# Two bites of TensorE in the short steps of the late attention, and scatters three in two steps

## The chip, the cores and the metric

The kernel runs on one core of a Trainium2 chip. The metric is the device time of one execution in microseconds, as the median of several runs. A core has five engines with queues of their own: TensorE (matmuls), VectorE, ScalarE, GpSimd (POOL) and SyncE (SP, which here only issues DMAs). They meet through semaphores alone.

## The reference

Four batches of 1024 tokens with 256 features go through four blocks in a row, each with a layer norm in front and added to its input: attention, a mixture of experts, a short convolution over the batch axis, and the mixture of experts again.

```python
x = x + attn(layernorm(x))     # 16 heads of 16; scores ** 4, causal, divided by their sum
x = x + ffn(layernorm(x))      # top 6 of 16 experts (176 wide), and a shared expert (352 wide)
x = x + conv(layernorm(x))     # taps from delta, alpha, beta, gamma; silu
x = x + ffn(layernorm(x))

# attn, for each head
a = tril(einsum('bhnd,bhmd->bhnm', q, k) ** 4)      # q, k: rotary, then a layer norm over the head
out = einsum('bhnm,bhmd->bhnd', a / a.sum(-1), v)
```

All is float32.

## The kernel before

**Tiling.** Tokens stand in tiles of 128 (`X`: 8 tiles by 4 batches). The experts' tokens form two groups: the first four tiles of every batch are group 0, the last four group 1. For each group a plan picks the experts (`plan`, line 324); a scatter (`scatter`, line 420) writes each token's normed row six times into a queue in DRAM (`xq`), sorted by expert, one indirect DMA of POOL (line 445) for 128 rows; then 111 tiles of that queue run through the experts (`stream`, line 1047), and the results are gathered back (line 1217). Group 0's queue is filled for the first time while the attention still runs.

**The attention.** It runs in 16 passes: first the queries 0 to 511 (`hf` 0) of eight pairs (four batches by two groups of eight heads), then the queries 512 to 1023 (`hf` 1) of the same eight. A pass has two halves `a` of four heads, and each half runs over the blocks of 128 keys, in the order of `turns` (line 856): 0, 3, 1, 2 for the first queries, and 0, 7, 1, 6, 2, 5, 3, 4 for the second. So there are 8 x 8 + 8 x 16 = 192 steps. A step has one block of keys `j` against at most 512 queries; behind the diagonal there are fewer, in the second half 384, 256 and 128 for `j` 5, 6 and 7.

In each step the loop (line 888) first issues the scores of the step two ahead (`scores`, line 719: four matmuls at line 727, two squarings on ScalarE at line 738, masks and the second power of one part on VectorE, lines 745 and 758); then the second power of the other part on ScalarE (line 896); then this step's weighing of the values (`weigh`, line 765: four matmuls at line 773, into one accumulator). A matmul of float32 shows as two in the profile, so a step has eight of line 727 and eight of line 773.

**Bites.** All other work of the attention is cut into generators, which stand in five lanes (`Bites`, line 45): two for the projection, rotation and norm of queries, keys and values of a pass to come, one for the layer norm and transposes of its input, one for the outputs (`gather_bites`, `project_bites`), and one, ROUTE, for the zero fill of the queues and then for the routing of group 0: logits, plan and scatters. A generator yields "pe" ahead of a piece that uses TensorE, "el" ahead of one that doesn't, and "gap" where it is to wait for the next step. `step(pe, counts)` goes through the lanes in order, runs up to `counts` pieces of each, and at most `pe` with TensorE in all. It is called twice in a step of the loop: with one "pe" and one piece a lane ahead of the weighing, and behind it with the arguments that the change touches. `ran` counts the "pe" pieces, and is taken before the first call. A scatter is an "el" of its own, so a step issues at most as many scatters as the two calls let ROUTE have pieces. ROUTE's routing is added (line 918) once the first queries' outputs are through.

In the second half the second call had one "pe" only if the first had found none (line 907):

```python
                    pe = 1 if hf == 0 or bites.ran == ran else 0
                    bites.step(pe, (2, 2, 1, 2, 1))
```

**Order.** TensorE, VectorE, ScalarE and SP run their instructions in the order in which the program issues them (`manual_schedule`). POOL is not among these engines; it has the scatters, and in the second half the copies of the values into `vB` (line 611), two a pass. The rows to scatter are normed into `sxn` for two tokens' tiles (12 scatters) at a time (line 429, by way of line 207); the next 12's rows are made six scatters ahead, in one of two buffers.

**What follows.** At the end of the loop the last outputs are drained, then what is left of ROUTE. Then the memory of the attention is given to the experts' weights and buffers: the first rows of the shared expert (`hxn`, line 973), its transposes (`hpt`, line 985), the loads of the weights (lines 940 to 956) and of the queue (`xg`, line 1062).

Of the kernel before, what the change touches and what calls it, by code (L numbers as in the profile page):

```python
# [99 lines left out]
def chain(*parts):  # L100
    for part in parts:
        yield from part
# [3 lines left out]
def block_kernel(  # L106
# [154 lines left out]
    plans = {}  # L261
# [46 lines left out]
    def prepare_all(g, pool, ps):  # L308

        for i in range(TG):  # L310
            yield "el"
            ln_stats(X[:, g * TG + i, :, :], mvs[g][:, 4 * i : 4 * i + 4, :], "r")
        yield "gap"
        yield "el"
        ln_root(mvs[g], rstds[g])
        yield "gap"
        yield "el"
        nc.vector.reciprocal(rstds[g], rstds[g])
        for i in range(TG):
            if i:  # L320
                yield "el"
            yield from logits_of(g, i, pool, ps)
# [148 lines left out]
    with ExitStack() as actx:  # L471
# [65 lines left out]
        def zero_fill():  # L537
            for q in xq:
                rows = q.rearrange("(p r) e -> p r e", p=P)
                for c in range(0, NTILE, LB):  # L540
                    yield "el"
                    nc.sync.dma_start(
                        out=rows[:, c : c + LB, :],
                        in_=zero[:, None, :].to_broadcast([P, LB, E]),
                    )
# [7 lines left out]
        def norm_bites(l, hf):  # L553

            xs = X[:, 4 * hf : 4 * hf + 4, l, :]
            yield "el"
            mv = small.tile([P, 4, 2], FP, tag="a_mv", name="a_mv")
            rstd = small.tile([P, 4], FP, tag="a_rstd", name="a_rstd")
            ln_stats(xs, mv, "a")
            yield "gap"  # L560
            yield "el"
            ln_root(mv, rstd)
            yield "gap"
            yield "el"
            nc.vector.reciprocal(rstd, rstd)
            xn = ap1.tile([P, 4, E], FP, name="xn")
            ln_apply(xs, xn, mv, rstd)
            xnT = ap2.tile([P, 2, 512], FP, name="xnT")
            xnT_of[l, hf] = xnT
            yield "gap"  # L570
            yield "gap"
            for k in range(2):
                yield "pe"
                pt = ps_m().tile([P, 512], FP, tag="m", name="pt")
                transpose4(pt, xn, slice(k * P, (k + 1) * P))
                nc.scalar.copy(xnT[:, k, :], pt)
# [188 lines left out]
        def weigh(u, hf, a, j, last, s2s):  # L765
            n0 = max(0, (j - 4 * hf) * P)
            if j == 0:
                accs[0] = PS["a"].tile([P, 512], FP, tag="acc", name="acc")
            acc = accs[0]
            va = vs_of[u, j // 4]  # L770
            for r in (2, 0, 1, 3):
                h = 2 * r + a
                nc.tensor.matmul(  # L773
                    acc[32 * r : 32 * r + 32, n0:512],
                    lhsT=va[:, j % 4, h * VW : h * VW + 32],
                    rhs=s2s[r // 2][:, r % 2, 0 : 512 - n0],
                    start=(j == 0),
                    stop=(j == last),
                )
            if j == last:  # L780
                o_sb = ap2.tile([P, 4, P], FP, name="o_sb")
                nc.scalar.copy(o_sb.rearrange("p t n -> p (t n)"), acc)
                return o_sb

        def gather_bites(u, hf, a, o_sb):

            yield "gap"
            yield "pe"
            l, gp = pairs[u]
            if gp == 0 and a == 0:  # L790
                at_of[l, hf] = ap2.tile([P, 4, E], FP, name="at")
            at = at_of[l, hf]
            po = ps_m().tile([P, 4, G, 32], FP, tag="m", name="po")
            for i in range(4):
                nc.tensor.transpose(
                    po[:, i, :, :].rearrange("p r d -> p (r d)"), o_sb[:, i, :], ident
                )
            rd = small.tile([P, 4, G], FP, tag="rd", name="rd")
            nc.vector.reciprocal(rd, po[:, :, :, D])
            nc.vector.tensor_mul(  # L800
                at.rearrange("p t (g r a d) -> p t g r a d", g=2, r=G, a=2)[:, :, gp, :, a, :],
                po[:, :, :, 0:D],
                rd[:, :, :, None].to_broadcast([P, 4, G, D]),
            )
# [32 lines left out]
        bites = Bites(5)  # L837
# [3 lines left out]
        def begin_chain(n):  # L841

            hf, u = passes[n]
            l, gp = pairs[u]
            if gp == 0:
                bites.need(NORM, (l, hf))
            bites.add(gp, qkv_bites(u, hf), n)
            if gp == 1 and n + 1 < len(passes):
                hf, u = passes[n + 1]
                l = pairs[u][0]  # L850
                bites.add(NORM, norm_bites(l, hf), (l, hf))
# [12 lines left out]
        def forward(i):  # L864

            n, a, j, last = steps[i]
            hf, u = passes[n]
            if a == 0 and j == 0:
                bites.need(pairs[u][1], n)
            if hf == 0 and a == 1 and j == 0:  # L870
                begin_chain(n + 2)
            if hf == 1 and u > 0 and a == 0 and j == 0 and n + 1 < len(passes):
                begin_chain(n + 1)
            return scores(u, hf, a, j, last)

        with tc.manual_schedule(engines=ORDERED):
            with tc.tile_pool(name="ps_s", bufs=2, space=PSUM) as s, tc.tile_pool(
                name="ps_a", bufs=1, space=PSUM
            ) as a, tc.tile_pool(name="ps_m", bufs=3, space=PSUM) as m:
                PS.update(s=s, a=a, m=m)  # L880
                bites.add(NORM, norm_bites(0, 0), (0, 0))
                begin_chain(0)
                bites.need(QKV0, 0)
                begin_chain(1)
                bites.add(ROUTE, taps(ap1, ps_m))
                bites.add(ROUTE, zero_fill())
                routed = False
                for s in range(-LOOK, len(steps)):
                    bites.begin()
                    new = []  # L890
                    ran = bites.ran
                    if s + LOOK < len(steps):
                        powers[s + LOOK], new = forward(s + LOOK)
                    bites.step(1, (1, 1, 1, 1, 1))
                    for part in later:
                        nc.scalar.activation(part, part, AF.Square)  # L896
                    later[:] = new
                    if s < 0:
                        bites.step(1, (2, 2, 1, 2, 1))
                        continue  # L900
                    n, a, j, last = steps[s]
                    hf, u = passes[n]
                    o_sb = weigh(u, hf, a, j, last, powers.pop(s))
                    if a == 1 and j == last:
                        weighed[0] = n

                    pe = 1 if hf == 0 or bites.ran == ran else 0
                    bites.step(pe, (2, 2, 1, 2, 1))
                    if o_sb is not None:
                        l, gp = pairs[u]  # L910
                        done = gather_bites(u, hf, a, o_sb)
                        if gp == 1 and a == 1:
                            done = chain(done, project_bites(l, hf))
                        bites.add(OUT, done)
                    if hf == 1 and not routed and not bites.lanes[OUT]:

                        routed = True
                        bites.add(ROUTE, prepare_all(0, ap1, ps_m))
                        bites.add(ROUTE, chain(plan(0, ps_m), scatter(0, ap2, 1)))
                bites.drain(OUT)  # L920
                bites.drain(ROUTE)


    with ExitStack() as fctx:
# [120 lines left out]
        bites = Bites(3)  # L1045
# [344 lines left out]
```

## Time and profile before

| | us |
|---|---|
| median of 3 runs | 2450.68 (2448.94 to 2451.34) |
| profiled execution | 2440.91 |
| its span, first to last instruction | 2439.2 |
| TensorE busy in the span | 2133.4 (87%), 10512 matmuls |
| ScalarE busy | 1240.8 (51%) |
| VectorE busy | 1110.1 (46%) |
| POOL busy | 846.5 (35%) |
| line 445, 384 scatters | 384.1, 1.00 each |
| line 727, score matmuls, 1024 of the group with the first queries' keys | 167.8 |
| line 773, weighing, 1024 of the group with the first queries' values | 124.5 |
| first scatter of group 0, start | 554.4 |
| last scatter of group 0, start | 721.1 |
| last weighing, end | 711.6 |
| first experts' matmul (line 1091) | about 805 |

The page of a profile gives each engine's busy time in 40 slices, the chain of waits that ended last (followed back from the last instruction through what released each one), the groups of instructions by line, and the idle time before them with what ended it. "Another core or an unknown queue" stands where the release fits no instruction of the profile. The ends of matmuls are modelled, so a wait for TensorE beyond its last recorded end falls under that name. The attention ends at 711.6 us; the rest is the shared expert of group 0, four streams of 111 tiles, and the last combine.

### The profile page before, as it was taken

What the parts mean: (1) busy time and instruction counts of PE and PEld (TensorE: products, weight loads), DVE (VectorE), ACT (ScalarE), POOL (GpSimd) and SP (SyncE); (2) the same over time, 40 slices, a digit from 0 to 9 for tenths busy, and PEclk for the clock granted to TensorE, in tenths of its full rate; (3) what the DMA queues carried; (4) which work ended last, traced back from release to release, by engine and by line L of the source; (5) the groups of instructions that cost most, each with busy time, mean ns of one, the idle gap of its engine ahead of it and who ended that gap; (6) DMA issues with size and microseconds to landing.
All of it is one profiled execution on the core that took longest, in us unless ns stands there. A gap on an engine that the chain in (4) does not pass through costs nothing.

```text
span 2439.2 us, 32993 instructions
## 1 busy us (share of the span) xinstructions
PE 2133.4 (87%) x10512; PEld 1328.8 (54%) x10512; DVE 1110.1 (46%) x2599; ACT 1240.8 (51%) x2774; POOL 846.5 (35%) x903
## 2 busy tenths in 40 slices
PE   5899999997769988899899987988998799999755
PEld 2344433332225766677666655766665467777433
DVE  6888777884542341111465511146561113431244
ACT  4788888886651543345455423445552334555200
POOL 3222100006650026600554066155406625530365
PEclk8899999998889999999999998999999899999967
DMA  7900000002224134433444243344424336653233
GB/s 252 329 1 1 1 1 1 1 1 78 74 94 124 56 100 173 167 102 115 146 138 132 80 153 139 102 144 146 122 84 149 143 106 189 193 169 104 89 100 93
DMA packets 210214, 267.72 MB, mean 110 GB/s; under 512 B 23232, under 2 KB 185184, under 8 KB 210048
## 3 DMA queue, kind: packets, MB, share of 16 engines
q1 hardware_dynamic: 168544, 161.43, 20.5%
q0 software_dynamic: 37056, 100.91, 12.8%
q10 hardware_dynamic: 4448, 3.28, 0.5%
q8 instruction: 91, 1.49, 0.3%
q14 instruction: 75, 0.61, 0.1%
HBM read 123.72 MB, written 141.82 MB: 109 GB/s over the span
## 4 chain that ended last, share of the span: by engine, by line
PE 67%; DVE 15%; ACT 7%; another core or an unknown queue 6%; issue 4%; DMA 1%; POOL 0%; ACTq 0%; DVEq 0%; POOLq 0%
PE pgu L1091 19%; PE py L1114 15%; PE ps L727 5%; PE pht L1105 4%; PE pxt L1075 4%; PE pg L1010 3%; PE acc L773 3%; PE pu L1010 3%; PE pj L600 3%; PE po L1030 2%; DVE s L758 2%; ACT s L738 2%; DVE X L1201 1%; DVE s L745 1%
## 5 line engine op out<-in xcount | busy, mean ns | idle before, releaser
L1091 PE MATMUL pgu<-wgu,xgT 128*128 x1776 | 617.3, 471 | 4.5 <-DVE hbuf L1100 3.2
L1217 POOL DMA_INDIRECT yg<-yq,sloti x384 | 381.6, 994 | 589.4 <-DMA yq<-yo 325.5
L445 POOL DMA_INDIRECT xq<-sxn,sloti x384 | 384.1, 1000 | 517.1 <-ACT xgT L1077 362.9
L1100 DVE TENSOR_TENSOR hbuf<-hbuf,pgu 128x176 f32<-128x176 f32 x444 | 149.0, 336 | 746.4 <-ACT hbuf L1099 616.4
L1091 PEld LDWEIGHTS pgu<-wgu,xgT 128*128 128x128 f32 x1776 | 345.8, 196 | 140.8 <-issue 22.7
L1099 ACT ACTIVATE hbuf<-pgu 128x176 f32<-128x176 f32 x444 | 142.1, 320 | 393.3 <-PE pgu L1091 273.0
L738 ACT ACTIVATE s<-ps 128x1024 f32<-128x1024 f32 (+3 forms) x384 | 291.9, 816 | 83.4 <-PE ps L727 53.6
L1114 PE MATMUL py<-w2a,hT 128*128 x888 | 282.7, 401 | 35.3 <-issue 24.4
L1123 ACT COPY yo<-py 128x256 f32<-128x256 f32 x444 | 166.5, 375 | 250.9 <-PE py L1114 141.6
L1114 PE MATMUL py<-w2b,hT 128*128 x888 | 274.3, 392 | 0.0
L1105 PE MATMUL pht<-ident,hbuf 128*128 128x128 f32 x888 | 175.4, 280 | 64.6 <-ACT hT L1107 57.7
L1105 PEld LDWEIGHTS pht<-ident,hbuf 128*128 128x128 f32 x888 | 124.0, 144 | 195.8 <-ACT hT L1107 75.8
L758 DVE TENSOR_TENSOR s<-s 128x1024 f32<-128x1024 f32 (+3 forms) x176 | 177.8, 1010 | 74.0 <-ACT s L738 65.9
L1201 DVE SCALAR_TENSOR_TENSOR X<-yg,top,X 128x256 f32<-128x256 f32 x384 | 185.4, 483 | 42.5 <-DMA yg<-yq,sloti 33.4
L1077 ACT COPY xgT<-pxt 128x256 f32<-128x256 f32 x444 | 170.0, 383 | 41.0 <-remote 9.3
L1114 PEld LDWEIGHTS py<-w2b,hT 128*128 128x128 f32 x888 | 175.1, 197 | 25.5
L1107 ACT COPY hT<-pht 128x256 f32<-128x256 f32 x444 | 166.1, 374 | 35.6 <-PE py L1114 13.4
L727 PE MATMUL ps<-q,kA 32*128 32x512 f32 (+3 forms) x1024 | 167.8, 595 | 17.8 <-ACT s L738 7.6
L1075 PE MATMUL pxt<-ident,xg 128*128 128x128 f32 x888 | 174.5, 279 | 9.7 <-issue 5.3
L896 ACT ACTIVATE s<-s 128x1024 f32<-128x1024 f32 (+3 forms) x208 | 169.5, 824 | 15.1 <-DVE s L745 15.1
L1114 PEld LDWEIGHTS py<-w2a,hT 128*128 128x128 f32 x888 | 138.4, 196 | 48.1 <-issue 28.4
L773 PE MATMUL acc<-s,vA 128*32 128x512 f32 (+3 forms) x1024 | 124.5, 552 | 16.8 <-ACT s L896 14.5
(165 smaller groups left out, 2311.0 us busy)
## 6 DMA issues: line engine op xcount, KB each, us to landing
xg<-xq SPq DMA_DIRECT2D x148, 384.0 KB
yq<-yo SPq DMA_DIRECT2D x148, 384.0 KB
xq<-zero SPq DMA_DIRECT2D x74, 384.0 KB
xq<-sxn,sloti POOLq DMA_INDIRECT x384
yg<-yq,sloti POOLq DMA_INDIRECT x384
wgu<-in_w SPq DMA_DIRECT2D x4, 1408.0 KB
X<-in_x SPq DMA_DIRECT2D x8, 512.0 KB
out<-X SPq DMA_DIRECT2D x8, 512.0 KB
```

The costliest lines, as they stand in the source:

```text
L445: d = nc.gpsimd.indirect_dma_start(out=xq[g][:, :], out_offset=bass.IndirectOffsetOnAxis(ap=sloti[:, c + i, k : k + 1], axis=0), in_=xs[:, ...
L727: nc.tensor.matmul(tiles[h // 2][:, h % 2, 0:nq], lhsT=kt[32 * h : 32 * h + 32, (j % 4) * P : (j % 4 + 1) * P], rhs=qT[u, hf][a][32 * h : ...
L738: nc.scalar.activation(s2[:, :, 0:nq], tiles[pr][:, :, 0:nq], AF.Square)
L758: nc.vector.tensor_mul(part, part, part)
L773: nc.tensor.matmul(acc[32 * r : 32 * r + 32, n0:512], lhsT=va[:, j % 4, h * VW : h * VW + 32], rhs=s2s[r // 2][:, r % 2, 0 : 512 - n0], st ...
L1075: nc.tensor.transpose(pt[:, k, :], xg[c][:, k * P : (k + 1) * P], ident)
L1077: nc.scalar.copy(xT[c], pt)
L1091: nc.tensor.matmul(pg, lhsT=xT[c][:, k, :], rhs=wgu_f[k][:, bass.ds(vals[0] * (2 * FI), 2 * FI)], start=(k == 0), stop=(k == 1),)
L1105: nc.tensor.transpose(pt[:, k, :], hbuf[c % 4][:, k * P : (k + 1) * P], ident)
L1114: nc.tensor.matmul(py, lhsT=hT[c][:, k, :], rhs=w2_f[k][:, bass.ds(off[c] * E, E)], start=(k == 0), stop=(k == 1),)
L1201: nc.vector.scalar_tensor_tensor(X[:, t, l, :], yg[:, k, :], top[:, i, k0 + k : k0 + k + 1], X[:, t, l, :], op0=ALU.mult, op1=ALU.add,)
L1217: nc.gpsimd.indirect_dma_start(out=yg[:, k, :], out_offset=None, in_=yq[g][:, :], in_offset=bass.IndirectOffsetOnAxis(ap=sloti[:, i, k0 + ...
```

## The change

Two arguments of the second call in the attention's loop change.

```diff
-                    pe = 1 if hf == 0 or bites.ran == ran else 0
-                    bites.step(pe, (2, 2, 1, 2, 1))
+                    pe = 1 if hf == 0 else (2 if j > 4 else 1) - (bites.ran - ran)
+                    bites.step(pe, (2, 2, 1, 2, 1 if 0 not in plans or s % 2 else 0))
```

In the second half a step whose weighing has key block 5, 6 or 7, thus at most 384 queries, may run two pieces with TensorE over both calls; the others one, as before. And once the plan of group 0 is there (`plans[0]` is set by the last piece of `plan`, line 416), the second call gives ROUTE a piece in odd steps alone, so that with the first call's piece there are three scatters in two steps instead of four. With the order of `turns`, odd steps are those with key blocks 7, 6, 5 and 4. No instruction is added or removed.

## The prediction

> **What bounds the kernel now.** I read the granted clock first (one core, 0.938 on the mean), then the page's slices, then the stages that the change touches.
>
> ```profile
> PE   5899999997769988899899987988998799999755
> POOL 3222100006650026600554066155406625530365
> PEclk8899999998889999999999998999999899999967
> ```
>
> A slice is 61 us. TensorE is at nine tenths from the third slice on, except in slices 10 to 12 (549 to 732 us): the end of attention, in which POOL issues the 96 scatters of the first group. There the clock falls too. The stretches of 20 us say more:
>
> ```profile
> core 0: us, PE busy (x) PEld busy (x) DVE busy (x) ACT busy (x) POOL busy (x), PEclk, DMA share, GB/s
> 560.00:580.00 20.00, 18.67 (x116) 6.04 (x108) 10.48 (x18) 16.53 (x22) 15.62 (x14) 0.86 0.27 93
> 580.00:600.00 20.00, 13.82 (x47) 4.32 (x44) 3.51 (x8) 5.79 (x9) 14.19 (x14) 0.74 0.28 98
> 620.00:640.00 20.00, 19.00 (x135) 8.25 (x132) 16.04 (x29) 17.15 (x25) 14.32 (x12) 1.00 0.21 73
> 640.00:660.00 20.00, 13.86 (x93) 4.40 (x86) 9.25 (x15) 13.22 (x18) 15.43 (x16) 0.94 0.28 97
> 660.00:680.00 20.00, 11.11 (x43) 3.01 (x46) 3.37 (x5) 6.07 (x8) 9.38 (x10) 0.50 0.19 67
> ```
>
> From 580 to 600 and from 660 to 680 TensorE, VectorE and ScalarE all but stop together, and POOL alone goes on. The chain of waits there:
>
> ```profile
> by line: another core or an unknown queue 74.0%; ACT s L738 14.1%; PE ps L727 7.1%; ACT s L896 5.4%; issue 1.0%; ACTq L738 0.1%
> ...
> 653.18 4.83 another core or an unknown queue
> 658.03 0.60 ACT s L738
> ...
> 661.05 9.65 another core or an unknown queue
> 670.72 1.02 ACT s L738
> ```
>
> ScalarE's squaring waits for TensorE's semaphore, which comes 4 to 11 us after the modelled end of the score matmuls. Nothing in the program makes TensorE late: its matmuls have started. What the stalls share is a long unbroken run of indirect DMAs on POOL, one every 1.28 us: 32 from 554.4 to 598.2, stalled from about the 18th, and 36 from 622.3 to 672.1, stalled from about the 25th; each stall ends within 2.5 us of its run. I take the run of scatters to be the cause. The same label has 20.2% of the chain from 1400 to 1520 (81 scatters, 13.5 in 20 us), 3.3% from 900 to 1040 (92, 13.1 in 20 us), and no share that shows from 1160 to 1320 (88 gathers, 11 in 20 us): it depends on the rate.
>
> **Size of the stalls.** Line 773 has eight matmuls in each of 192 steps, so the start of its every eighth matmul dates the steps. Eight late steps, with one bite among them, take 2.16, 2.31, 2.95, 2.74, 3.17, 3.04, 3.05 and 2.66 us for keys 0, 7, 1, 6, 2, 5, 3, 4 (steps 182 to 189): 22.1, or 44.2 for a pass of 16. Passes 2 to 5 of the second half (steps 80 to 143) take 52.1, 50.3, 52.3 and 51.4 with 58 bites: 29.4 over 4 x 44.2, 0.51 a bite. Steps 149 to 189 take 159.4 against 113.4 of base and 17 x 0.51 = 8.6 of bites: **37 us too much**. The chain's own label from 545 to 725, 16.4% of 180 = 29.5 us, is the lower bound; the rest is the half clock behind each stall.
>
> **What the change moves.** Before, a second-half step runs one bite of TensorE. By the lanes' rules, counted through the loop, the routing's bites come last in line: its last (line 413) falls in step 147, and the trace has that matmul at 543.0, where step 147 starts. The first two scatters are in step 149, two a step follow, 86 are issued in the loop and 10 behind it. After, a step with key 5, 6 or 7 (at most 384 queries) has room for two. Counted in the same way, no bite of a query, key and value chain moves but the queries' turn (one step earlier); gathers, output projection and routing move up. Line 413 falls in step 119, 28 steps x 3.22 = 90 us earlier (about 453 us). Scatters run from step 121 to 184, three in two steps: all 96 in the loop, 8 steps to spare. That is 9.3 in 20 us, below the gathers that show no stall.
>
> **Cost of each part.** *Scatters, rate.* The 37 us go as far as the stalls do. POOL may run ahead within a chunk of 12, because the next rows (line 207) come six scatters before their use: 12 x 1.28 = 15.3 us of issue, then a pause, as 12 now have 8 steps = 25.8 us. Only the first two chunks can make one run of 24, and a copy of vB (line 611) that waits for a projection may split it. The former runs stalled past 18 and 24; the third run (689.2 to 722.1, 24 scatters) has its loop steps at their base. Unknown: what is left. From below 0 (the gathers' row); from above the 37 us over the 68 scatters of the two stalled runs, 0.54 x 96 = 52. I take 3, near the gathers' row, with 12 in a run.
>
> *Scatters, end.*
>
> ```profile
> 721.14 0.97 POOL L445 DMA_INDIRECT xq<-sxn,sloti  x1 [0.30 <-issue]
> 723.88 9.07 DVE L207 TENSOR_SCALAR hxn<-X,mvs,rstds 128x256 f32<-128x256 f32 x7 [10.16 <-DMA xq<-sxn,sloti]
> ...
> 724.35 3.50 POOL L954 MEMSET w2b<- 32x4096 f32 x1 [2.24 <-issue]
> ...
> 734.52 1.97 PE L189 MATMUL hpt<-ident,hxn 128*128 128x128 f32 x8 [16.13 <-DVE X L833]
> ```
>
> The shared expert's first rows wait until 723.88 for the landing of the last scatter. Without it the next is late: the last output projection's matmuls, recorded until 718.4. So 723.9 - 718.4 = 5.5, taken as **5**; from 0 (if something else holds the memory) to 10.2 (the whole wait). The two memsets of 3.5 us behind, beside which two of the vector instructions take 3.80 and 3.68 instead of 0.41, come earlier with them and stay. SP's queue loads of group 0, and the weights behind these, move up alike: the weights are first needed at 805.
>
> *Bites.* Nothing is added. In steps 78 to 148 an even step (512 queries) with one bite lies 0.51 over its base, an odd one 0.22 (32 steps each); nine bites move from even to odd: 9 x 0.29 = **2.6 gained**. Eighteen steps get two, of which the trace of this half has none. If nothing hides the second, it costs its TensorE or ScalarE time: six queries' turns at 1.62, six gathers and three turns of line 816 at 0.66, three output projections at 1.92, 21.5 us, less 18 x 0.51 where they were: +12. From the other side -5. Behind a waiting bite on TensorE's in-order queue stands that step's weighing; three buffers of ps_m and the gaps in the bites keep two steps between a bite and its reader. I take the row of odd steps.
>
> *Vector work beside scatters.* The eight pairs of rows (2 x 0.41) and the planning move whole into fuller passes: 0; the rows cost 8 x 0.8 = 6.4 more if they were free before and are not now, and save as much in the opposite case.
>
> **A rule against it.** The trace has the 96 scatters in
>
> ```profile
> L445 POOL DMA_INDIRECT xq<-sxn,sloti x96 | 104.0, 1083 | 74.0 <-DVE sxn L207 45.7 <-issue 24.9 <-DMA xq<-sxn,sloti 2.7
> ```
>
> so the mean is 0.11 above the 0.97 of an undisturbed one: 10 us in all, under the pauses. The Trainium skill, page "SBUF — State Buffer", section "Who interferes with whom", says that VectorE and GpSimd hold a shared port pair for a whole instruction, and that one with two SBUF inputs, such as line 758's product, shuts out a GpSimd instruction that reads SBUF. If each scatter lost one such product (1.23 us by the trace), 96 would take 96 x 2.5 = 240 us against the 71 steps x 3.2 = 227 that the loop then has left: by the rule, as an estimate, 13 us would hang over behind the attention and the 5 at its end would not come, 2427 in all; by the row the sum is the one below.
>
> **Sum.** Against the profiled execution's own 2440.9 us (span 2439.2): -37 + 3 - 5 - 2.6 = -41.6, so 2399.3. The median of the runs is 2450.7, 9.8 above the profiled one; the same on top gives **2409**.
>
> **Rivals.** *Half stays* (16%): the first run of 24 and a chunk or two stall as the former first run did, about 17 us: 2409 + 14 = 2423, 2418 to 2438. For it: 13.1 in 20 us still costs 3.3% at 900 to 1040. Against: 9.3 is lower.
>
> *The stalls' cause is not the scatters, or the rule changes nothing* (10%): 2450.7 - 5 - 2.6 = 2443, 2440 to 2450. For it: the third run did not stall, and the label names no queue. Against: before 545, where POOL issues no indirect DMA, the label has no share that shows.
>
> *Each scatter costs, wherever it stands* (slower, 10%): spread over 64 fuller steps, the 96 cost the upper bound, 0.54 each = 52 us instead of 37, and at eight chunks that is 6.5 a chunk. 2450.7 + 15 - 7.6 = 2458. It decides from 45 us of stalls, 0.47 a scatter. For it: the third fill, paced over the tiles, loses 24 us in 81 scatters (0.30) without long runs. Against: 0.05 at 900 to 1040, and 0 with the gathers.
>
> The forecast itself (64%): 2398 to 2421, from 2450.7 - 37 - 10.2 - 5 = 2398.5 with no stall left and both other terms at their best, to the 12 more for second bites that nothing hides.
>
> **Range and chances.** About 0.2% (5 us) is what can be told from no change here. The forecast and half stays are faster: 80%, and of the third rival two parts in ten: faster 0.82, same 0.08, slower 0.10. The range, 2396 to 2438, holds these two (80%) and stops short of the last two rivals; its lower end is the forecast's best with 2 us for reading the steps.
>
> **What would show it.** Line 413 near 453 us and the scatters from about 465 to 657; pauses of POOL between chunks of 12; no "unknown queue" over 1 us in the chain of the attention; passes of 50 to 52 us to the end; the weighing over at about 675 instead of 711.6; hxn waiting for TensorE, not a DMA, and hpt some 18 us after the last weighing instead of 23. Wrong if ScalarE still waits for late score matmuls while POOL pauses, or if steps with two bites take over 1 us more than their base.

## The result, and the profile after

The changed kernel takes 2466.77 us (median of 17 runs, 2453.66 to 2486.21) against 2448.94 for the kernel before in the same session (17 runs): a ratio of 1.0063, 95% interval 1.0043 to 1.0082. It is slower by 0.6%, where 2409 us was forecast. The profiled execution took 2456.46 us, with a span of 2454.7.

The first slices of the page of the changed kernel, 61 us each:

```profile
PE   5899899887889998899999977999997799999754
POOL 3222000244421026601553166155316615530455
PEclk8999999888989999999999988999999999999877
```

Line 413 starts at 460.7 us and the scatters run from 471.2 to 692.0: they begin near the forecast's place (453; 465 to 657) and end 35 us behind it. POOL's work did move to slices 8 to 12, thinner than before. But TensorE, with 9, 9, 7, 7 and 6 tenths there before, now has 8, 8, 7, 8 and 8: the hole was spread, not closed. The stretches of 20 us of the same execution (busy us of TensorE's matmuls, its weight loads, VectorE, ScalarE and POOL; granted clock; DMA):

```profile
core 0: us, PE busy (x) PEld busy (x) DVE busy (x) ACT busy (x) POOL busy (x), PEclk, DMA share, GB/s
440.00:460.00 20.00, 15.44 (x92) 4.76 (x84) 19.42 (x32) 14.04 (x16) 0.00 (x0) 0.91 0.00 0
480.00:500.00 20.00, 18.69 (x80) 5.29 (x73) 7.86 (x18) 11.70 (x16) 12.91 (x13) 0.61 0.23 79
560.00:580.00 20.00, 16.91 (x88) 5.57 (x84) 12.87 (x22) 11.14 (x16) 8.92 (x10) 0.76 0.18 60
600.00:620.00 20.00, 14.31 (x64) 4.63 (x66) 7.17 (x11) 13.33 (x16) 3.40 (x4) 0.66 0.07 23
680.00:700.00 20.00, 15.59 (x92) 4.81 (x84) 7.93 (x14) 12.43 (x17) 10.53 (x10) 0.75 0.21 72
```

There are two different losses. In the first row POOL does nothing and VectorE is full: TensorE waits for VectorE. In the others POOL issues scatters in runs of 12, VectorE is one to two thirds busy, and the clock is at 0.61 to 0.76. From 480 to 500 TensorE counts as busy for 18.69 us but shows only 80 matmuls there, against 138 in the same stretch of a version below: long matmuls, at half the clock up to 495.4. The chain of waits of the changed kernel names the second loss:

```profile
484.09 3.05 another core or an unknown queue
487.17 1.03 ACT s L738
...
534.74 2.57 another core or an unknown queue
...
597.39 3.26 another core or an unknown queue
...
602.12 2.12 another core or an unknown queue
```

The first three pieces begin 10 to 13 us behind the start of a run of 12 (471.2, 524.2, 586.9). So the stalls are there again at the rate at which none was forecast, and the squaring of line 738 still waits for late score matmuls. The end did gain. The shared expert's first rows, in the timeline of the changed kernel (start, us; in brackets the idle time and who ended it):

```profile
733.86 2.35 DVE L207 TENSOR_SCALAR hxn<-X,mvs,rstds 128x256 f32<-128x256 f32 x7 [1.37 <-PE pt L189]
737.83 3.51 POOL L954 MEMSET w2b<- 32x4096 f32 x1 [44.34 <-DMA xg<-xq]
738.41 1.10 PE L189 MATMUL hpt<-ident,hxn 128*128 128x128 f32 x8 [0.78 <-DVE X L833]
742.45 3.78 PE L1010 MATMUL pg<-hxT,sh 128*128 128x512 f32 x4 [2.94 <-ACT hxT L986]
```

The rows wait for TensorE and not for a DMA, as forecast, and the memsets now stand behind them. From the last weighing's end to pg it is 12.5 us (729.9 to 742.4), where it was 24.7 (711.6 to 736.3).

Dated by the starts of line 773's matmuls as in the forecast, the attention's steps take (us; the last column is from the start of the last step's weighing to pg, the shared expert's first matmul; the runs e1 to e15 are described below):

```
steps                    64-79 80-95 96-111 112-127 128-143 144-159 160-175 176-190   64-190  to pg
before                    56.7  52.1   50.3    52.3    51.4    65.8    50.2    58.3    436.9   26.6
after                     55.6  56.6   55.0    66.2    60.2    64.8    56.0    45.6    459.9   14.5
before, no scatters  e3   55.6  54.5   51.9    52.3    51.4    51.8    48.9    40.1    406.6   13.5
after, no scatters   e4   55.5  53.8   55.3    60.5    54.2    51.7    52.1    40.1    423.3   13.5
rate alone           e2   56.7  52.1   50.3    52.3    51.4    59.4    49.4    39.9    411.4   51.1
bites alone          e1   56.6  53.2   57.0    59.4    65.3    68.4    50.7    39.8    450.5   14.5
after, paced         e5   55.6  53.8   56.9    59.1    54.2    51.5    52.1    40.1    423.3   13.5
no scat., plan later e8   55.5  56.6   55.0    51.8    54.0    52.6    50.8    40.1    416.3   13.5
before, paced       e14   56.7  52.0   50.3    52.3    51.4    53.5    51.7    47.7    415.6   29.6
all three edits     e15   55.5  56.6   54.9    52.0    52.7    52.7    50.4    39.9    414.6   14.7
```

Where nothing differs (steps 80 to 95 of before and e3), two executions are up to 2.4 us apart. The attention is 22.9 longer (459.9 - 436.9) and its end 12.2 shorter; the rest of the 15.5 between the two profiled executions (+9 behind pg, -4.6 ahead of step 64) is the spread of single executions.

### The profile page after: what moved, and what is told of

It reads as the page before. It is cut to its first block, busy times and chain, and to the rows that moved or that the text cites. A ratio compares the mean times of both kernels' runs of the same rounds, so it can differ in the third digit from the quotient of the medians.

```text
span 2454.7 us, 32993 instructions
## 1 busy us (share of the span) xinstructions
PE 2140.0 (87%) x10512; PEld 1328.0 (54%) x10512; DVE 1105.1 (45%) x2599; ACT 1241.5 (51%) x2774; POOL 847.6 (35%) x903
## 4 chain that ended last, share of the span: by engine, by line
PE 71%; DVE 12%; ACT 7%; issue 5%; another core or an unknown queue 4%; DMA 1%; POOL 1%; ACTq 0%; DVEq 0%; SPq 0%; POOLq 0%
PE pgu L1091 20%; PE py L1114 15%; PE ps L727 7%; PE pxt L1075 4%; PE pht L1105 4%; PE acc L773 4%; PE pj L600 3%; PE pu L1010 3%; PE pg L1010 3%; PE po L1030 3%; ACT s L738 2%; DVE s L758 1%; DVE X L1201 1%; PE pl L286 1%
```

## The experiments

**Runs 1 to 4: each part alone, and both kernels without group 0's scatters.** The first two take one line of the change each; the last two leave the scatters out.

```diff
 e1  pe = 1 if hf == 0 else (2 if j > 4 else 1) - (bites.ran - ran)
     bites.step(pe, (2, 2, 1, 2, 1))
 e2  pe = 1 if hf == 0 or bites.ran == ran else 0
     bites.step(pe, (2, 2, 1, 2, 1 if 0 not in plans or s % 2 else 0))
 e3, e4 (line 445, in before and after)
+                if group == "scatter0":
+                    continue
```

> Only the two bites in short steps; scatters stay at two a step. The plan is ready as early as in the changed kernel, so the scatters run from step 121 to 168, all in the loop. Theory A (the loss is in the scatters: every run of them holds TensorE up, wherever it stands, and more so beside fuller steps): about as slow as the changed kernel, 2460 to 2470, most of the excess in steps 121 to 168. Theory B (the loss is in the bites: second bites and a planning packed closer together): also about 2465, but with steps 64 to 120 some 15 us longer than before and steps 169 to 191 clean. Theory C (the slower rate spreads the stalls over more passes, and the bites are neutral): near or below before, 2435 to 2450.

> Only the scatters three in two steps; bites as before. The plan is as late as before (step 147), so 65 scatters are in the loop from step 149 and 31 behind it instead of 10: 21 x 1.28 = 27 us more behind the attention, and some of the stalls in the loop may go. Theory A: a run of 12 stalls as well as a run of 36, so at most a third of the 37 us goes and the time is 2455 to 2470. Theory C or the forecast's own (a lower rate frees TensorE): stalls nearly gone, 2435 to 2445. Theory B: says nothing of this one beyond the 27 us.

> The kernel before without the 96 scatter DMAs of group 0's first fill (their normed rows are still made); the queue of group 0 holds its zeros in the first stream. All theories: the 37 us of stalls and the wait of 5 to 12 us behind the attention are gone, 2398 to 2410. If the time stays near 2449, the stalls of the attention are not the scatters' doing.

> The changed kernel without the same 96 DMAs. Against the kernel before without them: theory A the same within 4 us (bites neutral, as forecast -2.6); theory B 10 to 20 us slower, in steps 64 to 170 of the attention.

Measured against the kernel before (2436.2 us there): e1 1.0023 (1.0001 to 1.0045), e2 1.0000 (0.9983 to 1.0017), e3 0.9801 (0.9777 to 0.9826), e4 0.9880 (0.9853 to 0.9907).

This splits the result. Without scatters the change costs 19 us by the ratios (0.0079 x 2436) and 22.6 by the medians: that is the price of the bites, the planning that moves with them included, forecast as a gain of 2.6. The steps show 16.7 of it (423.3 - 406.6); the rest lies ahead of step 64 and behind pg in the two profiles, where the programs don't differ, and no run explains it. With scatters, they cost the kernel before 48.8 us (2436.2 - 2387.4), of which the profiles show 30.3 in the steps (436.9 - 406.6) and 13 at the end; they cost the changed kernel 41 (1.0063 x 2436 - 2410), of which 36.6 lie in the steps (459.9 - 423.3) and 1 at the end. So the slower rate gained nothing in the steps of the changed kernel. e1 says it once more: with the bites alone the scatters cost 27.2 there (450.5 - 423.3), less than with the slower rate added. Its time falls into the range of Theory C, but not for its reason, since the bites are not neutral (e4).

e2 is the surprise. In the kernel before, the slower rate does what was forecast: the scatters' cost in the steps falls from 30.3 to 4.8. But with the plan as late as before, 31 scatters are left behind the loop, as expected, and the end pays. In the timeline of e2:

```profile
726.62 0.45 PE L189 MATMUL hpt<-ident,hxn 128*128 128x128 f32 x1 [33.91 <-DMA xq<-sxn,sloti]
```

TensorE idles 33.9 us for the last scatter's landing; 51.1 us from the last weighing to pg against 26.6. What the rate gains, the end takes.

**Runs 5 to 8: what of the scatters delays TensorE, and where the price of the bites lies.**

```diff
 e5 (line 738; the scatters then wait for this squaring, by the program's own pacing of later fills)
-                nc.scalar.activation(s2[:, :, 0:nq], tiles[pr][:, :, 0:nq], AF.Square)
+                d = nc.scalar.activation(s2[:, :, 0:nq], tiles[pr][:, :, 0:nq], AF.Square)
+                pace["after"] = d.ins.name
 (behind the drain of ROUTE, ahead of the streams)
+                pace["after"] = None
 e6 (line 445)
+                if group == "scatter0":
+                    r0 = (c * TOPK + j) * P
+                    nc.sync.dma_start(out=xq[g][r0 : r0 + P, :], in_=xs[:, i, :])
+                    continue
 e7 (line 445)
+                if group == "scatter0":
+                    for _ in range(2):
+                        spare = pool.tile([P, E], FP, tag="spare", name="spare")
+                        nc.gpsimd.tensor_copy(spare, xs[:, i, :])
+                    continue
 e8 (e4, and in plan, ahead of pa)
+        if g == 0:
+            for _ in range(8):
+                yield "gap"
```

> The changed kernel with one dependency more for each scatter of group 0: it also waits for the newest squaring of scores (line 738) that had been issued before it, so that POOL cannot run a chunk of 12 back to back but issues about three in two steps (some 9 in 20 us). Theory A (TensorE's completions come late only while POOL issues indirect DMAs back to back): the stalls of the runs of 12 vanish, and the time falls to near the changed kernel without scatters, 0.988 of the kernel before, plus at most 0.2% of end: 0.988 to 0.992. Theory B (each scatter costs about 0.38 us of TensorE wherever it stands, 36.6 us over 96 in the changed kernel's steps): the time stays at that of the changed kernel, 1.006, or above it where POOL now waits.

> The changed kernel with the 96 scatters of group 0 replaced by 96 plain DMAs of the same rows, issued by SP at the same places and written to consecutive rows of the queue (the rows are not sorted by expert: this part of the computation is left out). The bytes moved are the same, and POOL issues nothing. Theory A (it is POOL's issuing of indirect DMAs that makes TensorE's completions late): no stalls, 0.988 of the kernel before, as without scatters. Theory B (it is the writing of 128 rows to DRAM and its semaphores): the stalls stay, 1.003 to 1.008.

> The changed kernel with each of the 96 scatters of group 0 replaced by two copies on POOL of the same 128x256 row block to a spare tile (about 0.4 us each by line 611's row): POOL is occupied at the same places and reads the same memory, and nothing is written to the queue (that part of the computation is left out). Theory A (indirect DMAs as such): no stalls, 0.988 of the kernel before. Theory B (POOL being occupied: the copies of values behind it, the memory port that it shares): 0.996 to 1.006, with late score matmuls as in the changed kernel.

> The changed kernel without group 0's scatters (left out of the computation, as in the fourth run), and with the planning held back by eight gaps ahead of its first matmul, so that its vector work falls into steps 122 to 127, behind the rotation and norm of that pass, and not beside them in steps 115 to 119. Theory A (of the 22.6 us that the bites cost, some 7 are the planning's vector work meeting a pass's rotation and norm on VectorE, in steps 116 to 119: 10.0 over base against 2.4 in the kernel before): 2403, 0.985 of the kernel before. Theory B (the bites' cost is the second bite in a step, some 1.2 us each, wherever the planning stands): 2410, 0.988.

Measured (before 2435.6 there): e5 0.9899 (0.9879 to 0.9920), e6 0.9891 (0.9864 to 0.9919), e7 0.9908 (0.9879 to 0.9936), e8 0.9864 (0.9840 to 0.9887).

e5, e6 and e7 all land where e4 is. So the stalls need POOL's indirect DMAs, and need them close behind each other: the same bytes written by SP's DMAs cost next to nothing (426.7 us in the steps, against e4's 423.3), POOL as busy with copies costs nothing, and the same 96 scatters cost nothing once each one waits for a squaring of scores. That POOL was as busy is in its groups, first the changed kernel's from 440 to 740 us, then e7's from 440 to 700:

```profile
L445 POOL DMA_INDIRECT xq<-sxn,sloti x96 | 102.8, 1071 | 147.5 <-DVE sxn L207 120.7 <-issue 25.6 <-DMA xq<-sxn,sloti 1.2
```

```profile
L448 POOL COPY spare<-sxn 128x256 f32<-128x256 f32 x192 | 102.0, 583 | 114.0 <-DVE sxn L207 114.0
```

102.0 us against 102.8, in the same runs between the same waits for VectorE's rows. It also settles what the rule that the forecast weighed is worth here (the Trainium skill, page "SBUF — State Buffer", section "Who interferes with whom"). The page has VectorE and GpSimd share a port pair, and VectorE's products of line 758 stood beside these copies. The copies do take longer than undisturbed ones (0.58 us on the mean, against 0.40 of line 611's fastest): the 72 that overlap such a product take 0.83, the other 120 take 0.44, which agrees with the page. So POOL pays; TensorE doesn't: the steps take 424.2 us with them and 423.3 without.

The trace can be read for the same thing. TensorE's updates of the semaphore that ScalarE and VectorE wait for are recorded; counted are those that come more than 1 us behind the last modelled end of a matmul, from the first scatter of group 0 to 5 us behind the start of the last (without scatters, in the whole attention). In the last column a pause of POOL under 1 us counts as none:

```
                                       late  us in sum  long runs of scatters
before                                    9       26.5  32, 36 and 24
after                                    13       42.9  12
after, once more (e13)                   17       34.6  12
e1 bites alone                           14       34.4  24 and 12
e16 each sixth paced                     16       27.1  11 and 12
e2 rate alone                             4        8.9  24 and 12
e14 before, paced                         4        9.2  16, 12, 10, 14, and 20 at the end
e5, e15 paced at three in two steps       0          0  6
e3, e4, e6, e7, e8 no scatters            0          0  -
```

That the seven runs with none are not from sessions without stalls (there are such, see below) shows behind the attention: there, beside the scatters of later fills, each of these traces has 72 to 102 late updates.

e8 moves the planning's vector work behind the rotation and norm of the pass in which the change puts it. Steps 112 to 127 fall from 60.5 to 51.8, near the 52.3 that they take without the change, and the whole from 423.3 to 416.3. What collided there, in the timeline of VectorE in e4 (behind line 445 its lines are numbered two higher: its 760 is line 758):

```profile
452.51 0.57 DVE L395 TENSOR_TENSOR slot_at<-pb,run 128x256 f32<-128x256 f32 x1
453.12 1.76 DVE L397 TENSOR_TENSOR hot<-hot,slot_at 128x1536 f32<-128x1536 f32 x1
454.79 1.22 DVE L760 TENSOR_TENSOR s<-s 128x1024 f32<-128x1024 f32 x1
455.93 0.68 DVE L640 TENSOR_REDUCE h_sm<-m 128x32 f32<-128x512 f32 x1
456.64 0.69 DVE L641 SCALAR_TENSOR_TENSOR m<-h_sm,m 128x512 f32<-128x512 f32 x1
457.37 0.69 DVE L650 TENSOR_TENSOR m<-m 128x512 f32<-128x512 f32 x1
458.10 0.69 DVE L651 TENSOR_REDUCE h_vs<-m 128x32 f32<-128x512 f32 x1
458.70 1.74 DVE L400 TENSOR_REDUCE slot<-hot 128x96 f32<-128x1536 f32 x1
...
461.40 1.23 DVE L760 TENSOR_TENSOR s<-s 128x1024 f32<-128x1024 f32 x1
```

Between one product of the scores (line 760) and the next stand 5.4 us of norm and planning, and TensorE's weighing waits for the product: step 118 takes 8.7 us, against 4.2 in e3 and 4.7 in e8. The 21 us from 442 to 463, first of e4, then of e8:

```profile
442.00:463.00 21.00, 14.91 (x84) 4.29 (x76) 20.38 (x35) 12.97 (x16) 0.00 (x0) 0.79 0.00 0
442.00:463.00 21.00, 17.41 (x108) 5.17 (x100) 18.56 (x31) 17.98 (x23) 0.00 (x0) 0.92 0.00 1
```

VectorE is full in e4 (20.38 us) and has room in e8 (18.56), where TensorE runs 108 matmuls instead of 84.

**Runs 9 to 12, in a session without stalls.** One thing has to be known to read them: here the kernel before itself takes 2240 us. Up to TensorE's last matmul there is not one late update in the four traces, nor the label "another core or an unknown queue" in the chain of waits of the streams of experts, which has 17.3% of the kernel before's own from 1380 to 1520. The page of the last run (e18), from a session like it, shows it in TensorE's row, at nine tenths nearly throughout where the kernel before and the changed one have sevens and eights from slice 24 on:

```profile
PE   5899999999998999999999999899999999999865
POOL 3122100025552005730555047465505745530276
PEclk7999999999999999999999999999999999999988
```

```diff
 e9 (e5, and)
+        if g == 0:
+            for _ in range(5):
+                yield "gap"
...
-                    pe = 1 if hf == 0 else (2 if j > 4 else 1) - (bites.ran - ran)
+                    pe = 1 if hf == 0 else (2 if j > 4 and 0 not in plans else 1) - (bites.ran - ran)
 e10 (e5's edit in the kernel before)
 e11 (e5, with)
-                if pace["after"] is not None:
+                if pace["after"] is not None and (group != "scatter0" or j % 6 == 0):
 e12 (e4, with e9's rule for pe)
```

> Three edits to the changed kernel: every scatter of group 0 waits for the newest squaring (as in the fifth run); two bites in a step only until the plan is there, one afterwards; and five gaps more ahead of the planning's first matmul, so that its vector work falls into steps 118 to 122, mostly behind the rotation and norm of that pass. By a replay of the lanes the scatters are then issued in steps 125 to 188, none behind the loop. Theory A (the three costs add up: scatters nothing when they are paced, planning beside a pass's norm 7 us, second bites behind the plan 3 to 6): the fifth run less 10 to 13 us, 0.984 to 0.986 of the kernel before. Theory B (the fifth run's gain is all there is, because the pacing has taken the same slack): 0.990.

> The kernel before, with nothing changed but that every scatter of group 0 waits for the newest squaring issued before it; two are issued in a step of some 2.8 us, which leaves POOL pauses of 0.2 to 0.6 us at most, and 10 scatters remain behind the loop. Theory A (what stalls TensorE is a long run of scatters without a link to the steps; paced ones cost nothing): 30 us of stalls go, some of the 12 at the end stay, 0.984 to 0.989. Theory B (it is the density, 13 or more in 20 us, with or without the link): the stalls stay, 0.995 to 1.002.

> The changed kernel in which only each sixth scatter of group 0 waits for the newest squaring, so that POOL issues runs of 6 (6 x 1.28 = 7.7 us) with pauses between. Theory A (a run has to last some 10 us before TensorE's completions come late: in the changed kernel the slow steps begin 10 to 13 us behind the start of a run): no stalls, 0.990 as with each one paced. Theory B (each scatter back to back with another adds its share): half of the stalls remain, 0.996 to 1.002.

> The changed kernel without group 0's scatters (left out of the computation, as in the fourth run), and with two bites in a step only until the plan is there, one afterwards; the planning stays where the change puts it. Theory A (moving bites costs where they leave steps in which TensorE waits anyway: 2.8 us in steps 128 to 143 and 3.2 in steps 160 to 175, against the kernel before without scatters): 2404, 0.986. Theory B (those differences are noise of one profile, the planning is the whole cost): 2410, 0.988 to 0.989.

Measured (before 2240.3 there): e9 0.9981 (0.9968 to 0.9994), e10 1.0010 (1.0000 to 1.0020), e11 1.0023 (1.0009 to 1.0037), e12 0.9988 (0.9976 to 0.9999). None of them can be judged as its expectation meant it, because where nothing stalls there is nothing to save by pacing. (e11, with runs of 11 and 22 scatters, has no late update here, so such runs alone don't make one.) The steps of e12 can still be set beside e4's, since neither has scatters: 128 to 143 take 50.3 instead of 54.2, and 160 to 175 take 47.7 instead of 52.1, as low as in e3. (The two sessions can be compared where nothing stalls: e11 and e5 differ by 0.5 us over steps 64 to 190.) So the second bites behind the plan do cost some 8 us, as its Theory A had it (it said 6). The price of the bites in the steps, e4 against e3, is thus 8.2 in 112 to 127, where the planning stands; 2.8 and 3.2 in 128 to 143 and 160 to 175, by the bites behind the plan; and 3.4 in 96 to 111, which no run separates.

**Runs 13 to 16: the open ones once more, in one session,** where the kernel before takes 2450.2.

> The changed kernel as it is. If the kernel before takes about 2240 us in these runs (completions of TensorE are not late there): Theory A (the price of the bites, 17 to 22 us, stands by itself, and the change's only gain is 5 to 12 us at the end): 1.003 to 1.006. Theory B (the change loses through the scatters' stalls alone): 0.995 to 0.999. If it takes 2430 us or more: 1.004 to 1.008 as before, with eight stalled runs of 12.

> The kernel before, each scatter of group 0 waiting for the newest squaring. Where the kernel before takes about 2240 us, 1.000 to 1.002 as in the tenth run. Where it takes 2430 or more: Theory A (paced scatters cost nothing, even at two a step): 0.984 to 0.989. Theory B (13 or more scatters in 20 us stall TensorE with or without the link to the steps): 0.995 to 1.002.

> The kernel of the ninth run (paced scatters, two bites only until the plan is there, planning five gaps later). Where the kernel before takes about 2240 us, 0.997 to 0.999 as there. Where it takes 2430 or more: Theory A (the costs add up): 0.984 to 0.986. Theory B (the pacing alone is the gain): 0.990.

> The kernel of the eleventh run (only each sixth scatter waits, so runs of 6). Where the kernel before takes about 2240 us, 1.002 as there. Where it takes 2430 or more: Theory A (a run has to last some 10 us before completions come late): 0.990. Theory B (each scatter back to back adds its share): 0.996 to 1.002.

Measured: e13 1.0071 (1.0050 to 1.0092), e14 0.9919 (0.9892 to 0.9946), e15 0.9812 (0.9789 to 0.9835), e16 1.0043 (1.0026 to 1.0061).

e13 repeats the result. e14 lies between its two theories, and its trace says why: at two scatters a step of some 2.8 us POOL has next to no pause, so runs of 16, 12, 10 and 14 scatters remain in the loop, and one of 20 at its end. Those of 10 and 14 have late updates (646.4; 670.8 and 672.2), the others none. A stretch with the run of 12 and one with that of 14, and then the second stretch in e15, the version told of below, also with 12 scatters in 20 us:

```profile
core 0: us, PE busy (x) PEld busy (x) DVE busy (x) ACT busy (x) POOL busy (x), PEclk, DMA share, GB/s
600.00:620.00 20.00, 20.00 (x138) 9.02 (x138) 18.81 (x33) 17.26 (x24) 14.07 (x13) 1.00 0.24 83
660.00:680.00 20.00, 16.78 (x101) 5.07 (x100) 9.36 (x16) 14.06 (x20) 12.12 (x12) 0.83 0.23 79
660.00:680.00 20.00, 18.08 (x126) 5.63 (x127) 10.71 (x17) 17.40 (x24) 12.95 (x12) 1.00 0.21 72
```

The second stretch has room in any case (in e3, without scatters, these steps show 18.09 us and 123 matmuls in the 20 us from 650). But steps 177 and 185 of e14, behind the runs of 10 and 14, take 5.9 and 5.8 us where e3 has 2.3, and that is 7 of the 9 us below. So the rate in 20 us is not what decides, and the length of a run alone isn't either: here 16 and 12 pass and 10 stalls. The scatters' cost in the steps is 9.0 us (415.6 - 406.6), and the end still waits for the ten left over (29.6 us to pg).

e16 did not do what it was made for. A chunk's first scatter runs, then the other eleven back to back (527.1 to 540.9, for one): by the time POOL came to the seventh, its squaring was long done. So it tells nothing of runs of six; with runs of 11 it stalls like the changed kernel (460.5 us in the steps).

e15 is the version to which the experiments point (e9's three edits), and it beats both kernels: 2405.6 us, 44.6 below the kernel before; the ratio is below what its Theory A expected (0.984 to 0.986). Its stretches where the changed kernel's were shown:

```profile
core 0: us, PE busy (x) PEld busy (x) DVE busy (x) ACT busy (x) POOL busy (x), PEclk, DMA share, GB/s
480.00:500.00 20.00, 20.00 (x138) 7.51 (x132) 16.02 (x36) 18.22 (x29) 12.26 (x13) 1.00 0.20 67
600.00:620.00 20.00, 19.61 (x129) 8.22 (x126) 19.57 (x32) 16.85 (x23) 10.39 (x10) 1.00 0.19 66
```

From 480 to 500 POOL issues as much as in the changed kernel (12.26 us against 12.91), and TensorE runs 138 matmuls instead of 80. e5, which has the pacing alone, issues 13 scatters there and runs 124. What the pacing changes for the scatters is two things at once: no more than six stand together, and each waits for a squaring of scores, so that it can start at another moment of TensorE's work. No run separates the two.

**Runs 17 and 18: the same idea in the streams.** e17 is e15 with the two fills beside the streams spread over more tiles; e18 is e15 once more.

```diff
 e17 (line 437)
-                if j % n == 0:
+                if j in (0, 3, 5, 8, 10) if n == 3 else j % n == 0:
                     yield "el"
```

> The kernel of the fifteenth run, and the scatters of the two later fills that are issued beside the streams three a tile (in about 1360 to 1500 and 1790 to 1930 us) issued in groups of 3, 2, 3, 2 and 2 a tile, so over 40 tiles instead of 32. Theory A (runs of 12 with 3.5 us between them delay TensorE's completions there as in the attention, and shorter runs do not): 15 to 50 us less than e18 where the kernel before takes 2430 or more, 0.960 to 0.975 of it. Theory B (the fills take the same time, since POOL is the limit either way, or the last scatters come too late for the next stream): within 5 us of e18, or slower.

> The kernel of the fifteenth run once more, for e17 to be compared with on one chip: 0.981 of the kernel before where that takes 2430 us or more, 0.998 where it takes 2240.

Measured (before 2241.9: again a session without late updates): e17 1.0012 (1.0001 to 1.0023), e18 0.9983 (0.9970 to 0.9996). Where nothing stalls, spreading the fills loses 5.7 us against e18. Whether it gains where they stall stays open.

## Why the prediction was wrong

**The cause of the stalls: right.** Without scatters not one update of TensorE is late in the attention, and 30.3 us leave the steps. In steps 149 to 189, where the forecast read 37, it is 33.6 (159.4 - 125.8): without scatters they lie 12.4 over base, where 8.6 were allowed for bites.

**"What is left: 3, with 12 in a run": the first failed step.** It is 36.6 us (459.9 - 423.3), well inside the bounds of 0 and 52 that the forecast itself had set. The low end was taken for two wrong reasons. The rows by which a run of 18 or 25 was still harmless were read as a threshold; in the changed kernel the stalls begin 10 to 13 us behind the start of a run, with eight to ten scatters issued. And the gathers, 11 in 20 us without a stall, were taken as a rate; what e14 and e15 show is that 12 scatters in 20 us stall in one case and not in the other. The rule about the rate did hold in the kernel before (e2, 4.8 us left, with runs of 12), whose late passes have less other work; that it didn't hold in the changed kernel with the same runs of 12 is measured, why is not.

**The end, "5": mis-sized.** It gained 12.2. The bound of 10.2 counted the whole wait of VectorE for the last landing; what it left out is that the two memsets behind it slowed the rows, which took 9.07 us; in the changed kernel they stand ahead of the memsets and take 2.35.

**The bites, "2.6 gained": the second failed step, and the one that gives the sign.** With the planning they cost 19 to 23 us, 16.7 of it in the steps; without it 9.7 (e8 against e3, 416.3 - 406.6), inside the upper bound of 12. Had they been neutral, the scatters and the end would have left a gain of some 6 us (36.6 - 30.3 - 12.2). The working priced the steps that receive a bite, and that part was good: in e4 the 13 two-bite steps of 78 to 148 lie 0.48 over their base. It never priced the steps that lose one: it took them to fall to base. In the same stretch e4 has 22 steps without a bite, at 1.23 (even) and 1.04 (odd) over base, more than the 0.57 and 0.29 of one-bite steps in e3; the kernel before had seven such steps, at 1.01 and 0.89, which could have been read. Part of the even ones' excess is the planning (step 118 alone 5.5): in e8 they are at 0.43, the odd ones still at 0.88. So a bite taken out gave little back in the even steps and nothing in the odd ones. Why they take longer is not shown; TensorE's waits in the slow steps of e8 without a bite end with ScalarE's squarings.

**"Vector work: 0, at most 6.4": failed.** The rows did cost nothing, but the planning, named in the same breath, met a pass's norm on VectorE and cost 7 (e8). These 7 are part of the 19 to 23 above.

**The rivals.** "Each scatter costs, wherever it stands" came nearest, 2458. That is luck in part: its price, 0.54, was 0.38 (36.6 / 96), which is below its own point of decision at 0.47, and "wherever it stands" is false, since paced they cost nothing; it too had the bites as a gain. The forecast is off by 58 us, outside its range: 34 in the scatters that are left (36.6 instead of 3), 7 in stalls that were smaller than thought (30 instead of 37), 19 to 25 in the bites and the planning, less 7 at the end.

**What was to show it.** Line 413, the scatters' start, POOL's pauses and hxn's wait for TensorE came as written; hpt came 8.5 us behind the last weighing instead of 18, but that weighing ended at 729.9 instead of 675. One of the two signs of failure came, ScalarE waiting for late score matmuls also while POOL pauses (604.2 and 605.0, behind the run of 587 to 602); with it came passes of 55 to 66 us instead of 50 to 52. The other did not: two-bite steps of 78 to 148 lie 0.48 over base in e4 and 0.86 in the changed kernel, not over 1.

## What to carry to other kernels

Price a move at both ends: taking work out of a step gains nothing if the step is as long without it, so the row to look for is that of steps without it. When a queue of one engine delays another, a lower mean rate may not help; try to tie each of its instructions to the progress of the one that suffers. In the changed kernel the slower rate gained nothing in the steps, the dependency 36 us. And when a gain is given back at the end (e2), count what the slower pace leaves behind the loop.

## What the hardware showed that was not expected

- In the sessions with stalls TensorE's completions come late in the attention, by up to 6.6 us behind the last matmul's modelled end, around runs of ten and more indirect DMAs of POOL, and in none of the runs in which POOL copies or SP writes the same rows instead. Of 48 late ones (in separate bursts, seven traces) 20 fall within 0.1 us of a landing on the scatters' semaphores, against 9 to 25% of all of TensorE's updates. What they share on the chip no run shows. The Trainium skill, page "DMA: Bandwidth & Descriptors", section "Latency and other measured facts", places the descriptor rings of DMAs issued by GpSimd in SBUF and guesses at contention on their ports, as a reason why two DMA engines are slow; it says nothing of TensorE. That SP's DMAs don't disturb would agree with such a cause, and no run here tests it.
- Most late completions go with the half clock: the changed kernel's granted clock drops to 0.5 at 539.8, 601.2, 635.4 and 690.0 us, each within 3 us of the first late one (537.3, 600.6, 634.2, 690.3), and score matmuls of 512 queries then take 1.06 to 1.22 us instead of 0.59 to 0.69. But the half clock also comes without them: at 478.4, 6 us ahead of the first stall shown, and in e4, which has none, seven times from 477.9 to 693.0. The Trainium skill, page "TensorE: Matmul & The Clock Gate", section "What's actually happening", has half the clock after an idle window of some 3.4 us; that each such stretch here is 3.4 us long or a multiple (up to 17.1 from 478.4) agrees with a window of this length.
- It isn't there in every session. The kernel before takes 2436 to 2450 us in some sessions and 2240 to 2242 in others, with no late update in the six traces from the latter; there e15's kernel gains 0.2% instead of 1.9%. The record has the same chip number for sessions of both kinds (2 for 2436 and 2240, 1 for 2450 and 2242); what differs between them no run shows.
